# A list schedule's key for TensorE products that use a part of the array

## Chip, cores and metric

The kernel runs on one core of one Trainium2 chip. The metric is the device time of one execution in microseconds (us); lower is better. Times before are the median, the lowest and the highest of three runs.

## What is computed

A decoder of four layers, each with a self-attention block, a cross-attention block and a feed-forward block, on 32 sequences of 64 tokens (2048 tokens of 256 float32 values) and a context of 128 values a token. Every block has the form x = x + f(layernorm(x)), and the twelve f differ:

```python
x = x + _L0_attn_ref(_layernorm(x), wq, wk, wv, wo, ...)        # rope attention, 32 heads of 64, 8 kv heads
x = x + _L0_xattn_ref(_layernorm(x), ctx_1024, mask, ...)       # 16 heads of 128 on the context
x = x + _L0_ffn_ref(_layernorm(x), ...)                         # relu^2 dense and a mixed projection
x = x + _L1_attn_ref(_layernorm(x), ...)                        # Mamba-2 mixer, 32 heads
x = x + _L1_xattn_ref(_layernorm(x), ctx_1024, ...)             # 16 heads of 128, q and k normed
x = x + _L1_ffn_ref(_layernorm(x), ...)                         # 8 experts, top 2
x = x + _L2_attn_ref(_layernorm(x), ...)                        # Mamba-2 mixer, 8 heads
x = x + _L2_xattn_ref(_layernorm(x), ctx_1024, ...)             # 16 heads of 16
x = x + _L2_ffn_ref(_layernorm(x), ...)                         # one binarized projection
x = x + _L3_attn_ref(_layernorm(x), ...)                        # fp4-quantized, 32 heads of 8
x = x + _L3_xattn_ref(_layernorm(x), ctx_1024, pos, ...)        # axial rope, 32 heads of 8
x = x + _L3_ffn_ref(_layernorm(x), ...)                         # 64 experts, top 6, capacity 128, and a shared one
```

## The kernel before

**Tiles and stages.** The tokens stand in SBUF as 16 tiles of 128 (two sequences each). A unit works one block on one tile, or on a pair of tiles. `GROUPS = (8, 6, 2)` splits the tiles into three groups. `body` records the stages so that the early, wide stages of one group are woven (`weave`) with the late, narrow stages of the group before; the first group's early stages have nothing beside them, and the last group's late ones run beside the queued experts of layer 3. Every operation is only recorded: `Recorder.add` notes the engines that could run it, the tiles that it reads and writes, and so on whom it depends.

**The planner.** `Order.run` then decides, by list scheduling with its own table of durations (`duration`), which operation goes next and on which engine; `issue` writes out the instructions in that order. All instructions of the profile therefore carry one line, L2411, and are told apart by the names of their tiles. The order is fixed before the kernel runs: each engine takes its instructions strictly in it and waits on semaphores.

In each step `run` looks, for each engine, at the first 32 ready operations in the order of recording, gives each a key, and takes the lowest key over all engines (the earlier recorded one if keys are equal). The names that matter:

- `now` is when the engine is free, `since` when the inputs and a free slot are there, `start` the later of both.
- `o.soft` is the readiness plus a margin, if an input comes from another engine: `SLACK = {"tensor": 2.0, "vector": 0.5, ...}` us. The plain key is `max(now, o.soft, since)`. So an operation whose input has only just been planned is passed over while another has waited longer.
- `part` rounds the contraction and the output rows of a product up to 32, 64 or 128: the rows and columns of TensorE's 128x128 array that it uses. `self.part` is the part of the last product planned. A product of another part has `SWITCH = 0.1` us added to key and cost.
- `self.pos[o.at]` is the place of an operation in the recorded order, in us of planned TensorE work. `first` is the place of the oldest product that could start now. A product of the set part over `NEAR = 10` us behind `first` has `SWITCH` added to its key too.
- `fill` puts in a product that nobody reads (`spare_mm`) where TensorE would idle for over 1.6 us. `may_open` sees to it that buffers do not run out. PSUM has 8 slots, tag `mm`.

**Products that use a part.** Scores and outputs of attention heads are small, and several lie beside each other in the array:

- 128\*64: `cross_scores` (32 products a tile), `small_values`, `heads_mm` and the outputs of small heads
- 64\*64: `cross_out`, the outputs of L0's attention, `ssm_heads_mm` (32 products a group of heads)
- 32\*128: the scores of L0's attention (64 products a tile); 32\*64: `small_scores`
- 128\*32: sums of squares for L1's cross-attention and the mixers, the experts of layer 3

Their inputs come from ACT and DVE, piece by piece: `cross_out`, for one, takes each half of the transposed probabilities when it has been copied out of PSUM into `turn_b`.

Of the kernel before, what the change touches and what calls it, by code (L numbers as in the profile page):

```python
# [462 lines left out]
def duration(engine, method, args, kw):  # L463

    out = kw["out"] if "out" in kw else args[0]
    if method in DMA:
        return 0.45 if engine == "sync" else 1.28
    views = [v for v in [*args, *kw.values()] if isinstance(v, View)]
    n = max(v.size() for v in views)
    if engine == "tensor":  # L470
        k, m = part(method, args)
        if method == "transpose":
            return 0.109
        n = args[2].size()
        if m == 128:
            return max(0.223, n * 0.00167 + 0.004) if k > 32 else max(0.056, n * 0.00053)
        if k == 128:
            return max(0.058, n * 0.00083 + 0.003) if m == 64 else max(0.055, n * 0.00043 + 0.008)
        return n * 0.00042 + 0.002 if k == 64 else n * 0.00021 + 0.001
    small = any(v.size() == 1 and v.n > 1 for v in views) and n > 1  # L480
    psum = any(v.t.psum for v in views)
    full = sum(all(s for s, _ in v.dims) and v.size() == n for v in views[1:])
    if engine == "vector":
        if not psum and method in ("tensor_scalar", "tensor_copy", "tensor_scalar_add", "tensor_single_scalar"):
            return 0.16 + n * 0.00052 + 0.11 * small
        if method.startswith("reduce") and views[1].dims[-1][0] > 1:
            return 0.15 + n * 0.0017
        return 0.15 + n * 0.00104 + 0.06 * small
    if engine == "scalar":
        if method == "activation":  # L490
            return (0.17 if psum else 0.205) + n * 0.00083 + 0.18 * (small and psum)
        return 0.16 + n * 0.00084 + 0.1 * small
    if method == "memset":
        return 0.2 + n * 0.00066
    if ALU.pow in args:
        return 0.4 + 0.157 * n
    if method == "tensor_copy":
        return 0.25 + n * 0.001
    return 0.14 + n * (0.00174 if full < 2 else 0.0022)
# [27 lines left out]
class Order:  # L527
# [81 lines left out]
    def run(self):  # L609
        ready = {e: [] for e in self.ENGINES}  # L610

        def enter(op):
            for e, _ in op.ways:
                bisect.insort(ready[e], op, key=lambda o: o.at)

        for o in self.ops:
            if o.waits == 0:
                enter(o)
        done, oldest, result = [False] * len(self.ops), 0, []
        while not all(done[oldest:]):  # L620
            limit = self.pos[oldest] + self.horizon
            best = None
            for e in self.ENGINES:
                now, seen, first = self.free_at[e], 0, 1e9
                for o in ready[e]:
                    if self.pos[o.at] > limit or seen == 32:
                        break
                    seen += 1
                    since = o.ready
                    opens = [t for t in o.tiles if t.slot is None and t.tag in self.slots]  # L630
                    if opens:
                        if any(not self.free[t.tag] for t in opens):
                            continue
                        since = max([since] + [self.free[t.tag][0][0] for t in opens])
                    start = max(now, since)
                    method = next(m for w, m in o.ways if w == e)
                    cost = duration(e, method, o.args, o.kw)
                    key = max(now, o.soft, since)
                    if e == "tensor":
                        if start == now:  # L640
                            first = min(first, self.pos[o.at])
                        if part(method, o.args) != self.part:
                            key += SWITCH
                            cost += SWITCH
                        elif self.pos[o.at] > first + NEAR:
                            key += SWITCH
                    if e == "scalar":
                        table = TABLES.get(getattr(o.args[2], "name", "") if method == "activation" else "", 0)
                        if table and table != self.table:
                            key += 1.3  # L650
                            cost += 1.3
                    if e == "vector" and self.until["gpsimd"] > start and combines(o, e, method):
                        cost += min((1 - BESIDE) * (self.until["gpsimd"] - start), cost / BESIDE - cost)
                    if len(o.ways) > 1 and self.elsewhere(o, e, since, start + cost):
                        continue
                    if best is not None and (key, o.at) >= best[0] and not (
                        o is best[1] and start + cost < best[3] + best[4]
                    ):
                        continue
                    if opens and not self.may_open(o):  # L660
                        continue
                    best = ((key, o.at), o, e, start, cost, opens)
                    if key <= now:
                        break
            assert best is not None, "nothing can go on"
            _, o, e, start, cost, opens = best
            filler = self.fill(o, start) if e == "tensor" else None
            if filler:
                o, start, opens = filler, self.free_at[e], []
                cost = duration(e, "matmul", o.args, o.kw)  # L670
            else:
                for w, _ in o.ways:
                    ready[w].remove(o)
            for t in opens:
                t.slot = self.free[t.tag].pop(0)[1]
            got = start + cost
            end = got if o.ways[0][1] in DMA else got - EARLY.get(e, 0.0)
            self.free_at[e] = end
            m = next(m for w, m in o.ways if w == e)
            if combines(o, e, m):  # L680
                self.until[e] = got
                if e == "gpsimd" and self.until["vector"] > start:
                    more = min(self.until["vector"] - start, cost) * (1 / BESIDE - 1)
                    self.free_at["vector"] += more
                    self.until["vector"] += more
            elif e in self.until:
                self.until[e] = 0.0
            if e == "scalar":
                m = next(m for w, m in o.ways if w == e)
                table = TABLES.get(getattr(o.args[2], "name", "") if m == "activation" else "", 0)  # L690
                self.table = table or self.table
            if e == "tensor":
                self.part = part(o.ways[0][1], o.args)
            lat = latency(e, o)
            if o.ways[0][1] in DMA:
                v = next(v for v in o.outs + o.ins if isinstance(v, View) and v.dtype != I32)
                self.moved = max(self.moved, got) + v.n * v.size() * 4 / 300e3
                lat = 2.0 + self.moved - got
            for t in o.tiles:
                t.left -= 1  # L700
                if t.left == 0 and t.tag in self.slots:
                    bisect.insort(self.free[t.tag], (got + lat, t.slot))
            for n in o.after:
                same = len(n.ways) == 1 and n.ways[0][0] == e and o.ways[0][1] not in DMA
                at = (start if e in ("tensor", "sync") else got + 0.03) if same else got + lat
                n.ready = max(n.ready, at)
                n.soft = max(n.soft, at if same else at + SLACK.get(n.ways[0][0], 0.0))
                n.waits -= 1
                if n.waits == 0:
                    enter(n)  # L710
            if not filler:
                done[o.at] = True
            while oldest < len(done) and done[oldest]:
                oldest += 1
            oldest = min(oldest, len(done) - 1)
            result.append((o, e))
        self.length = max(self.free_at.values())
        return result
# [1791 lines left out]
```

## Time and profile before

| | |
|---|---|
| median of 3 runs | 3109.91 us (3098.72 to 3110.64) |
| profiled execution | 3237.79 us |
| its span, first to last instruction | 3236.0 us |
| mean granted TensorE clock in it | 0.955 |
| TensorE busy, records | 3064.8 us (95%), 26996 |
| DVE, ACT, POOL busy | 66%, 45%, 44% |

The profile is one execution. A float32 product leaves two records on TensorE (PE), a transpose one. PEld is the loading of the stationary operand, which overlaps PE. The timeline merges neighbouring records of one kind: start, length, engine and line, operation, tiles, rows\*columns of the array in use, shape of the moving operand, and how many. Waits are gaps of an engine together with what ended them.

### The profile page before, as it was taken

How to read it: one execution, taken by the hardware profiler on the slowest of the kernel's cores; microseconds unless marked ns; L12 is line 12 of the kernel's file. 1: busy time of each engine (PE TensorE's matmuls, PEld its weight loads, DVE VectorE, ACT ScalarE, POOL GpSimd, SP SyncE). 2: the span in 40 equal slices, each digit the busy share in tenths (PEclk: the TensorE clock that was granted, in tenths of full speed). 3: DMA queues.
4: the chain of work that ended last, by engine and by line, in shares of the span. 5: the costliest groups of instructions: out<-in, count | busy, mean ns of one | idle time of the engine just before them, and what ended most of it. 6: DMA issues, size and time to landing. Idle time of an engine off the chain costs nothing.

```text
span 3236.0 us, 66753 instructions
## 1 busy us (share of the span) xinstructions
PE 3064.8 (95%) x26996; PEld 2440.0 (75%) x26996; DVE 2122.1 (66%) x5175; ACT 1452.6 (45%) x2696; POOL 1424.3 (44%) x1281
## 2 busy tenths in 40 slices
PE   8999999999999999999999999989999999987779
PEld 7878887777777787788777776667778777765557
DVE  5554357775556666755789876767547788685474
ACT  1224226675442232544565664653335665363341
POOL 4532143225544555226564465644434575353420
PEclk9989999999998998999999999998899999898689
DMA  4102320121521443111110100112561211222441
GB/s 152 33 3 118 127 77 25 51 82 56 217 88 44 128 152 102 50 44 55 33 34 23 63 5 20 70 55 86 175 226 50 74 53 49 77 77 83 128 158 37
DMA packets 112951, 257.01 MB, mean 79 GB/s; under 512 B 26309, under 2 KB 73688, under 8 KB 100228
## 3 DMA queue, kind: packets, MB, share of 16 engines
q1 hardware_dynamic: 97860, 204.73, 18.3%
q0 software_dynamic: 14784, 48.01, 4.4%
q8 instruction: 214, 3.51, 0.5%
q14 instruction: 93, 0.76, 0.1%
HBM read 177.34 MB, written 78.77 MB: 79 GB/s over the span
## 4 chain that ended last, share of the span: by engine, by line
PE 80%; DVE 9%; issue 3%; POOL 3%; ACT 2%; DMA 1%; another core or an unknown queue 1%; SPq 0%; DVEq 0%; ACTq 0%; POOLq 0%
PE L_xattn_mm L2411 13%; PE L_attn_mm L2411 9%; PE cross_out_mm L2411 9%; PE ssm_heads_mm L2411 9%; PE pair_mm L2411 8%; PE L_ffn_mm L2411 5%; PE rope_mm L2411 4%; PE turn_mm L2411 4%; PE L_block_mm L2411 3%; PE cross_scores_mm L2411 2%; PE L_experts_mm L2411 2%; DVE ssm_heads_b L2411 2%; PE L_dense_mm L2411 2%; PE heads_mm L2411 2%; PE small_scores_mm L2411 1%
## 5 line engine op out<-in xcount | busy, mean ns | idle before, releaser
L2411 PE MATMUL pair_mm<-norm_b,load_ssm_w 128*128 128x256 f32 x1280 | 307.4, 385 | 0.0
L2411 PEld LDWEIGHTS pair_mm<-norm_b,load_ssm_w 128*128 128x128 f32 x1280 | 236.3, 191 | 43.0 <-issue 9.7
L2411 ACT COPY turn_b<-turn_mm 128x512 f32<-128x512 f32 x259 | 143.1, 592 | 203.9 <-PE turn_mm L2411 186.7
L2411 ACT ACT_TABLE_LOAD x165 | 211.7, 1283 | 19.5 <-DVE ssm_heads_b L2411 4.0
L2411 POOL TENSOR_TENSOR norm_sm<-norm_sm,__init___consts 128x1 f32<-128x1 f32 (+1 forms) x142 | 89.5, 635 | 287.0 <-DVE norm_sm L2411 268.8
L2411 DVE SCALAR_TENSOR_TENSOR ssm_heads_b<-pair_mm,load_ssm_wp,ssm_heads_b 128x252 f32<-128x252 f32 (+2 forms) x480 | 198.2, 465 | 20.7 <-ACT ssm_heads_b L2411 19.0
L2411 POOL TENSOR_TENSOR L_xattn_sm<-L_xattn_sm,__init___consts 128x8 f32<-128x8 f32 (+2 forms) x62 | 179.6, 2904 | 69.5 <-DVE L_xattn_sm L2411 50.6
L2411 ACT COPY L_xattn_b<-L_xattn_mm 128x512 f32<-128x512 f32 x191 | 112.2, 590 | 216.8 <-PE L_xattn_mm L2411 213.7
L2411 PE MATMUL rope_mm<-norm_b,load_L_attn_w 128*128 128x128 f32 x1280 | 163.4, 283 | 2.1 <-DMA load_L_attn_w<-in_a_wk 1.2
L2411 PEld LDWEIGHTS rope_mm<-norm_b,load_L_attn_w 128*128 128x128 f32 x1280 | 154.3, 196 | 11.0 <-issue 6.1
L2411 PE MATMUL ssm_heads_mm<-load_ssm_w,ssm_heads_b 128*128 128x256 f32 x640 | 157.0, 387 | 0.3 <-DVE ssm_heads_b L2411 0.3
L2411 POOL TENSOR_TENSOR ssm_heads_b<-ssm_heads_b,ssm_heads_b 128x1024 f32<-128x1024 f32 x30 | 76.1, 2536 | 166.3 <-DVE ssm_heads_b L2411 141.5
L2411 PEld LDWEIGHTS ssm_heads_mm<-load_ssm_w,ssm_heads_b 128*128 128x128 f32 x640 | 117.4, 190 | 34.3 <-issue 19.2
L2411 DVE TENSOR_SCALAR norm_b<-__init___x,norm_sm,norm_sm 128x256 f32<-128x256 f32 x192 | 111.8, 599 | 47.8 <-POOL norm_sm L2411 26.1
L2411 DVE TENSOR_TENSOR rope_b<-rope_mm,__init___consts 128x512 f32<-128x512 f32 x160 | 104.9, 680 | 54.2 <-POOL L_attn_b L2411 14.7
L2411 PEld LDWEIGHTS L_xattn_mm<-norm_b,load_L_xattn_w 128*128 128x128 f32 x1024 | 123.0, 195 | 14.1 <-issue 10.1
L2411 PE MATMUL L_attn_mm<-load_L_attn_w,L_attn_b 128*128 128x256 f32 x512 | 126.9, 401 | 5.8 <-issue 5.6
L2411 PE MATMUL L_xattn_mm<-norm_b,load_L_xattn_w 128*128 128x128 f32 x1024 | 130.3, 281 | 1.2 <-issue 0.8
L2411 POOL DMA_INDIRECT slots<-norm_b,L_ffn_sm x84 | 87.7, 1044 | 96.7 <-issue 44.5
L2411 ACT ACTIVATE ssm_heads_b<-ssm_heads_b 128x512 f32<-128x512 f32 (+1 forms) x120 | 91.8, 772 | 78.5 <-DVE ssm_heads_b L2411 50.5
L2411 POOL TENSOR_TENSOR L_attn_b<-rope_b 128x256 f32<-128x256 f32 x128 | 92.7, 742 | 77.1 <-DVE rope_b L2411 41.0
L2411 PE MATMUL L_xattn_mm<-norm_b,units_L_xattn_w 128*128 128x128 f32 x1024 | 124.2, 278 | 0.0
(440 smaller groups left out, 7935.6 us busy)
## 6 DMA issues: line engine op xcount, KB each, us to landing
queue<-far_w SPq DMA_DIRECT2D x14, 1024.0 KB
L_block_w<-in_f_rows SPq DMA_DIRECT2D x16, 770.0 KB
load_ssm_w<-in_s_in SPq DMA_DIRECT2D x12, 1024.0 KB
parts<-far_w SPq DMA_DIRECT2D x10, 1024.0 KB
slots<-far_w SPq DMA_DIRECT2D x16, 548.0 KB
L_experts_b<-slots SPq DMA_DIRECT2D x32, 274.0 KB
units_L_xattn_w<-kept_x SPq DMA_DIRECT2D x8, 1024.0 KB
L_parts_b<-parts SPq DMA_DIRECT2D x14, 512.0 KB
```

Of the source, the lines that this page charges most:

```text
L2411: done = getattr(getattr(nc, e), method)(*map(real, op.args), **{k: real(v) for k, v in op.kw.items()})
```

## The change

One branch is added to the key of TensorE's products: a product of the part that is set, if it is no more than `NEAR` behind `first` and the part is not the whole array, gets its bare `start` as its key, so without the margin of `SLACK`. Nothing else is touched; operations, durations, slots and the keys of other engines stay.

```diff
                         if part(method, o.args) != self.part:
                             key += SWITCH
                             cost += SWITCH
                         elif self.pos[o.at] > first + NEAR:
                             key += SWITCH
+                        elif self.part != (128, 128):
+                            key = start
                     if e == "scalar":
```

## The prediction

> **What bounds the kernel now.** I read the page's busy times first, then the slices, then the chain, then TensorE's waits, and last its timeline.
>
> ```profile
> PE 3064.8 (95%) x26996; PEld 2440.0 (75%) x26996; DVE 2122.1 (66%) x5175; ACT 1452.6 (45%) x2696; POOL 1424.3 (44%) x1281
> PE   8999999999999999999999999989999999987779
> PEclk9989999999998998999999999998899999898689
> PE 80%; DVE 9%; issue 3%; POOL 3%; ACT 2%; DMA 1%; another core or an unknown queue 1%; SPq 0%; DVEq 0%; ACTq 0%; POOLq 0%
> ```
>
> TensorE is busy for 95% of the span and carries 80% of the chain that ended last; no other engine passes 66%. In the table of stretches it is busy for 1954.8 of the first 2000 us, for 746.1 of the next 800 and for 363.9 of the last 436. So in most of the span a nanosecond taken from TensorE's queue is taken from the end, and in the last 436 us only about five in six are. Its waits are small and scattered:
>
> ```profile
> PE L_experts_mm L2411 <- ACT L_experts_b L2411: 12.9, 5, 4.7
> PE norm_mm L2411 <- DVE norm_b L2411: 11.8, 7, 8.3
> PE turn_mm L2411 <- ACT heads_b L2411: 9.3, 7, 3.4
> ...
> PE small_scores_mm L2411 <- ACT keys_apart_b L2411: 5.5, 5, 2.2
> ```
>
> (total us, times, longest). All gaps of over 150 ns between TensorE's products add to 138 us; 48 of these stand ahead of products that use a part of the array. What remains to be gained is inside the 95%: how the products follow each other. The timeline shows it:
>
> ```profile
> 956.20 1.06 PE L2411 MATMUL L_xattn_mm<-L_xattn_b,__init___consts 128*32 128x512 f32 x6
> 957.19 0.77 PE L2411 MATMUL norm_mm<-__init___consts,norm_b 128*128 128x128 f32 x5
> 957.89 1.04 PE L2411 MATMUL L_xattn_mm<-L_xattn_b,__init___consts 128*32 128x512 f32 x2
> 958.87 0.44 PE L2411 MATMUL norm_mm<-__init___consts,norm_b 128*128 128x128 f32 x2
> 959.23 1.20 PE L2411 MATMUL cross_scores_mm<-L_xattn_b,L_xattn_b 128*64 128x64 f32 x32
> 960.36 0.33 PE L2411 MATMUL norm_mm<-__init___consts,norm_b 128*128 128x128 f32 x1
> 960.62 1.20 PE L2411 MATMUL cross_scores_mm<-L_xattn_b,L_xattn_b 128*64 128x64 f32 x32
> ```
>
> 128\*32 is rows\*columns of the array in use, the last number the records (a float32 product leaves two, a transpose one). Four products of 128\*32 belong together; three run, norm transposes of the full array come between, and the fourth follows. One lone transpose stands between two batches of cross_scores. Each such **break** changes the array's part twice.
>
> **The price of a change of part.** I took the distance from one record's start to the next over the whole timeline. After a 128x128 record of the full array the median is 109 ns if the next record uses the full array (6492 cases), 202 to 205 ns if it uses a part. After a 128x256 record it is 216 ns (5389 cases) against 309. Going back, 128x128 records of 128\*64 are left after 203 ns, and 128x256 ones of 128\*32 after 309. So a change costs 93 ns whatever the parts, and a break 2 x 93 = 0.187 us. In the order of issue there are 1121 changes: 1121 x 0.093 = 104 us, 3.2% of the span. The planner's own SWITCH is 0.1 us.
>
> **What the Trainium skill says.** "TensorEngine Tiling (Array Packing)", Tiling Modes, Key Properties: "Changing tiling mode (not just tile) drains the TensorE". The trace agrees and prices it at 93 ns. "TensorE: Matmul & The Clock Gate", Part 3, on what overlaps: products start and end strictly in program order, so a product that waits holds all behind it; the records here start in the order of issue, save neighbours a few ns apart. The same page, Part 1: an idle window of about 3.4 us can drop the clock. The page's mean granted clock is 0.955, and a late evacuation here costs waits of 0.3 to 3 us, so I charge no clock to the change.
>
> **The change, part by part.** It adds and removes no instruction: the same 26996 TensorE records, the same loads, weight loads, evacuations and DMAs. It alters the order that the planner writes out. Before, a product's key is its readiness plus a margin of 2 us if another engine made its input (SLACK), so within these 2 us a full-array product, at a penalty of only 0.1, is taken first, and the part is left. Now, while a part other than the full one is set, a product of this part that lies within 10 us of recorded TensorE work of the oldest product that could start (NEAR) has its bare start as key: it goes on at once.
>
> *How many breaks can close.* In the order of issue 194 breaks have the same part back within 2.2 us. I then followed the kernel's dependences through the trace for every return to a part: in 223 cases the planner's readiness of the first returning product lies before the end of the run that had been left; in the trace all but 4 of these inputs were indeed there, and those 4 were late by 2.6 us together. But NEAR bites: in 124 of the 223 an older stage has a product startable that lies more than 10 us back (typically 20 to 25, up to 110, since two streams of tiles are woven). 99 keep the new key, and in 78 of them the whole returning run does. By 400 us of the span these 78 are 17, 7, 8, 6, 8, 8, 9 and, to the end, 15: everywhere.
>
> *The sum.* 78 x 0.187 = 14.6 us. The 21 that return in part still change twice: nothing. A run that is lengthened by a half to one us sees further products become ready; I take a quarter more, 3.6 us (bounds: 0, and all 194 short breaks, 194 x 0.187 = 36 us in all). Scores and outputs that finish a batch earlier free their PSUM banks and start the softmax earlier; of TensorE's 138 us of gaps I take 2%, 3 us (bounds: 0 and 15). Against it:
>
> - *The lost margin.* Products now issue with nothing between planned readiness and turn. By the trace, where the old plan left 0.1 to 0.5 us, a quarter of the products had less than 0.28 us left and one in twenty none; where it left over 2 us nearly none waited. The 4 late of 223 give 2.6 x 99/223 = 1.2 us; products that get ready inside the run are worse known, and I add 2 us (bounds: 0 and 40, below). Queued behind such a product is all of TensorE, and behind it ACT's and DVE's evacuations.
> - *The full-array products pushed back* by up to 1 us keep their own margin of 2 us and feed engines that are 45% and 66% busy: nothing. Where that cover is missing, in the last 436 us, the chain goes through DVE and ACT and a push costs what it lasts: 15 breaks x at most 0.5 us, of which I take none, as much is finished earlier as later.
> - *DMA queues, SP and POOL*: their instructions are placed by other keys and move only with the plan; no load is late in TensorE's waits but one of 1.2 us. Nothing.
>
> Sum: -14.6 - 3.6 - 3 + 3.2 = -18 us. The profiled execution took 3237.8 us (span 3236.0), 4% over the median of the runs, 3109.91; the saving is in TensorE's cycles and I carry it over unscaled: 3109.9 - 18 = **3092 us**, -0.6%. About 0.5% (15.5 us) is what a measurement of this kernel can tell from no change; its three runs spread over 12 us.
>
> **The rivals.** *Runs that grow.* If each lengthened run meets the next piece and the oldest startable product moves up because batches finish, NEAR excludes less and most of the 194 short breaks close: -36, with the gaps -45: 3065. For it: 194 of the breaks are short. Against: the older stream's products keep becoming ready one by one.
>
> *Little closes, or the plan gives it back.* A list schedule answers a local gain with another order everywhere. If NEAR excludes as counted, no run grows and the plan's idle time rises by 8 us: -14.6 + 3.2 + 8 = -3: 3106. That the change hardly does what it says is this case.
>
> *Slower: TensorE waits for evacuations.* Place: the second half of a batch right behind its ACT or DVE copy (turn_b into L_attn_mm and cross_out_mm, ssm_heads_b into ssm_heads_mm, L_experts_b into L_experts_mm), where the margin had hidden the copy's own queue. Price: before products that the old plan gave less than 0.1 us after their inputs, the trace has 98 gaps of over 150 ns, 88 us in all, so 0.9 us each. The gain of 18 is gone from 20 such waits on, one in five closed breaks; 40 make +18 and, with an order that is worse in the last 436 us, +22: 3132. Against it: 4 late of 223. For it: a plan with no margin there has not been seen in this trace.
>
> **How the numbers follow.** The forecast case 0.43, its own range 3080 to 3103; runs that grow 0.15; little closes 0.24; slower 0.18. Faster by over 0.5%: three quarters of the forecast and the runs that grow, 0.33 + 0.15 = 0.48. Within 0.5%: the rest of the forecast and nearly all of the third, 0.32. Slower: 0.18 and what the third has beyond, 0.20. The range reaches from a little past the growing runs with the full bound for the gaps (-51) to the slower case: 3055 to 3135.
>
> **What would show it.** Right: in the changed kernel's timeline the changes of part fall from 1121 to 900 to 970, runs of 128\*64, 64\*64 and 128\*32 get longer (now 26, 26 and 8 records), TensorE's busy time falls by 15 to 20 us, and its waits on ACT rise by less than 5. Wrong on the count: fewer than 80 or more than 300 changes gone. Wrong on the margin: waits of cross_out_mm, L_attn_mm or ssm_heads_mm on ACT and DVE that grow by 20 us or more. Wrong on the rest: changes gone as forecast, busy time down, and the span not.

## The result, and the profile after

The changed kernel takes **3057.78 us** (3054.86 to 3059.14, four runs); the kernel before, run beside it, 3106.36. The ratio is 0.9844, with a 95% interval of 0.9824 to 0.9865: 48.6 us or 1.6% faster. The forecast was 18 us. The direction was right and the time lies inside the stated range, but the size was off by a factor of 2.7.

Where a kernel ran matters for the numbers below: beside the changed kernel and e1 to e4 the kernel before took about 3106 us, beside e5 to e18 about 3225, so every ratio is to the kernel before run beside it and profiles are compared only within one of these two sets. The profile that the prediction reads (3237.8 us) belongs with e5 to e18, the profile after with e1 to e4; e1 below is therefore a second profile of the kernel before. The two then read, e1 first (span, busy time, PE's slices and the granted clock):

```profile
span 3107.2 us, 66753 instructions
PE 3004.8 (97%) x26996; PEld 2405.3 (77%) x26996; DVE 2120.7 (68%) x5175; ACT 1450.7 (47%) x2696; POOL 1427.3 (46%) x1281
PE   8999999999999999999999999999999999998989
PEclk9989999999999899999999999999899999899989
```

and after:

```profile
span 3053.1 us, 66780 instructions
PE 2959.3 (97%) x27012; PEld 2401.8 (79%) x27012; DVE 2119.0 (69%) x5186; ACT 1443.4 (47%) x2690; POOL 1411.6 (46%) x1273
PE   8999999999999999999998999999999999998889
PEclk9989999999999999999999999999899999999999
```

The work is the same: 26996 records and eight more spare products of two records each. The span falls by 54.1 us, and PE's busy time alone by 45.5. So TensorE was not freed of waits in the first place; it does the same products in less time. DVE, ACT and POOL hardly differ. In PEclk there are 2 eights instead of 5; in the records the granted clock is either 1 or 0.5, and within the span it stood at 0.5 for 167 us in e1 and 143 us after.

Counted in the order of issue, changes of part fall from 1121 to 996. By the page's groups of TensorE (tiles, part, shape, records, busy us and mean ns), the two groups that fall most are the output of L0's attention and a sum of squares in L1's cross-attention, each with e1 first:

```profile
L2411 PE MATMUL L_attn_mm<-turn_b,L_attn_b 64*64 64x256 f32 x512 | 61.9, 433 | 7.0 <-ACT L_attn_b L2411 4.3 <-DVE L_block_b L2411 2.7
```

```profile
L2413 PE MATMUL L_attn_mm<-turn_b,L_attn_b 64*64 64x256 f32 x512 | 43.7, 396 | 0.2 <-DVE rope_b L2413 0.2
```

```profile
L2411 PE MATMUL L_xattn_mm<-L_xattn_b,__init___consts 128*32 128x512 f32 x128 | 39.9, 605 | 0.0
```

```profile
L2413 PE MATMUL L_xattn_mm<-L_xattn_b,__init___consts 128*32 128x512 f32 x128 | 32.6, 605 | 0.0
```

In the first, the same 512 records take 18.2 us less. By the times of the halved clock, 9.1 us of the 61.9 and 2.4 of the 43.7 are lost to it, so 11.6 us are left that have to do with the order. The timelines of the two show how. In e1:

```profile
55.83 0.65 PE L2411 MATMUL L_attn_mm<-L_attn_b,L_attn_b 32*128 32x64 f32 x10
56.42 0.65 PE L2411 MATMUL L_attn_mm<-turn_b,L_attn_b 64*64 64x256 f32 x4
57.00 0.67 PE L2411 MATMUL L_attn_mm<-L_attn_b,L_attn_b 32*128 32x64 f32 x16
57.60 1.09 PE L2411 MATMUL L_attn_mm<-turn_b,L_attn_b 64*64 64x256 f32 x12
58.62 0.66 PE L2411 MATMUL L_attn_mm<-L_attn_b,L_attn_b 32*128 32x64 f32 x12
59.21 0.78 PE L2411 MATMUL L_attn_mm<-turn_b,L_attn_b 64*64 64x256 f32 x4
...
60.28 1.09 PE L2411 MATMUL L_attn_mm<-turn_b,L_attn_b 64*64 64x256 f32 x12
61.30 0.67 PE L2411 MATMUL L_attn_mm<-L_attn_b,L_attn_b 32*128 32x64 f32 x16
```

and after:

```profile
53.90 0.65 PE L2413 MATMUL L_attn_mm<-L_attn_b,L_attn_b 32*128 32x64 f32 x10
54.48 2.85 PE L2413 MATMUL L_attn_mm<-turn_b,L_attn_b 64*64 64x256 f32 x32
57.26 1.56 PE L2413 MATMUL L_attn_mm<-L_attn_b,L_attn_b 32*128 32x64 f32 x46
```

The 32 records of 64\*64 stood in four pieces that took 0.65 + 1.09 + 0.78 + 1.09 us, between scores of 32\*128; now they are one run of 2.85 us, and the scores are one run too. The break was not only against the full array but between two small parts.

The second group falls by 7.3 us, none of it halved clock. Its records stand in 38 runs in e1 and 31 after. The timeline that the prediction shows has the reason: three products of 128\*32 (6 records) took 1.06 us, and the fourth, alone (2 records), 1.04. In both traces a run of two, four, six or eight records takes 1.04 to 1.07 us. The four write to different columns of the array, so a product that comes with its batch costs next to nothing, and one that comes alone costs the time of the batch.

### The profile page after: what moved, and what is told of

It is laid out like the page before. It is cut to its first block, busy times and chain, and to the rows that moved or that the text cites. A ratio compares the mean times of both kernels' runs of the same rounds, so it can differ in the third digit from the quotient of the medians.

```text
span 3053.1 us, 66780 instructions
## 1 busy us (share of the span) xinstructions
PE 2959.3 (97%) x27012; PEld 2401.8 (79%) x27012; DVE 2119.0 (69%) x5186; ACT 1443.4 (47%) x2690; POOL 1411.6 (46%) x1273
## 5 line engine op out<-in xcount | busy, mean ns | idle before, releaser
L2413 POOL TENSOR_TENSOR L_xattn_sm<-L_xattn_sm,__init___consts 128x8 f32<-128x8 f32 (+2 forms) x62 | 179.1, 2896 | 30.2 <-DVE L_xattn_sm L2413 28.9
L2413 POOL TENSOR_TENSOR ssm_heads_b<-ssm_heads_b,ssm_heads_b 128x1024 f32<-128x1024 f32 x28 | 69.8, 2494 | 159.9 <-DVE ssm_heads_b L2413 130.2
L2413 POOL TENSOR_TENSOR heads_b<-heads_b,heads_sm 128x1024 f32<-128x1024 f32 x50 | 95.8, 1923 | 72.8 <-DVE heads_sm L2413 70.1
L2413 PEld LDWEIGHTS L_xattn_mm<-norm_b,units_L_xattn_w 128*128 128x128 f32 x1024 | 117.8, 192 | 5.8 <-issue 3.8
```

Source lines behind the costliest of these rows:

```text
L2413: done = getattr(getattr(nc, e), method)(*map(real, op.args), **{k: real(v) for k, v in op.kw.items()})
```

## The experiments

### e1: the kernel before, a second profile

No edit. 

> The kernel before, word for word, for a second profile: the first one's span (3236 us) lies 4% over the median of its runs, at a mean granted clock of 0.955, and can't be laid beside the span after (3053 us, 0.977). Theory 1 (what is gained beyond the changes of part is TensorE waiting less): the gaps of over 150 ns stay near 138 us, against 81 after. Theory 2 (the first profile was a slow execution, and its gaps with it): a span of 3090 to 3110 us, a clock of 0.97 to 0.98, and gaps of 80 to 110 us.

It took 3109.0 us, span 3107.2. The gaps of over 150 ns between products are 89 us instead of the 138 of the first profile. Theory 2 holds: a good third of the gaps that the prediction read belong to where that profile was taken. Against 80.9 us after, TensorE's gaps explain 8 us of the gain and no more.

### e2: breaks closed by hand

```diff
+def close(order, far=2.2):      # while a run v of q's part is planned to start within 2.2 us of q's end,
+                                # with u between, and v's inputs and slots are planned before q ends:
...
+            new = before + v + u + [o for r in runs[k + 1 :] for o in r]
+            if merged(new):     # the other engines' orders as they are, and no cycle
+                pe = new
-    issue(tc, order.run(), Net.SLOTS)
+    issue(tc, close(order.run()), Net.SLOTS)
```

> The order of the kernel before, in which 127 breaks are closed after planning: the returning run is put right behind the run that it continues, if all its inputs from other engines and its slots are planned to be there, and the full-array products between come after it. Nothing else moves; DVE, ACT, POOL and SP keep their order. Changes of part 889 instead of 1121. If a change costs 93 ns and the lost margin nothing: 232 x 0.093 = 21.6 us less, a ratio of 0.993. If the drain is hidden or products wait without their margin: 0.998 to 1.005. If the gain after comes from closed breaks and whatever else they bring by themselves (it was 48.6 us for 125 changes, 0.39 us each), this kernel gains 90 us: 0.971.

3059.5 us, a ratio of 0.9842 (0.9813 to 0.9872): 47 us for 232 changes, 0.20 us each and not 0.093. The reordering on TensorE alone, with no new plan, is enough for a gain of this size. Gaps rose by 14 us (to 103.5): giving up the margin does cost, but little. So either the price of a change was wrong or closed breaks bring something more, and e5 measures the price.

### e5: the price of a change by itself

```diff
+        for visits in (1, 20, 40, 80):
+            for v in range(visits):
+                for k in range(160 // visits):
+                    full(k)
+                for k in range(320 // visits):
+                    small(k)
```

> The kernel before, with four stretches of products behind its last one that nobody reads. Each stretch has the same 160 products of the full array (128 columns moving) and the same 320 of 64x64 (64 moving, four places of the array in turn), in 1, 20, 40 and 80 visits to the small part: 1 or 2, 40, 80 and 160 changes of part in all. Nothing in them waits for another engine. If a change costs the 93 ns that I read off the step across it, the last stretch is 158 x 0.093 = 14.7 us longer than the first. If it costs what the closed breaks gave back, 0.2 us, 32 us longer, and the 20 and 40 visits lie 8 and 16 us above the first. In between, the difference is the waits or the clock.

The four stretches as windows (length, then PE and PEld busy with records; next to nothing runs on the other engines, and the clock is full):

```profile
3221.20:3273.67 52.47, 46.31 (x961) 45.58 (x959) 0.42 (x1) 0.00 (x0) 0.00 (x0) 1.00 0.03 10
3273.67:3325.81 52.14, 52.14 (x966) 48.38 (x961) 0.00 (x0) 0.00 (x0) 0.00 (x0) 1.00 0.01 3
3325.81:3385.01 59.20, 59.20 (x966) 51.68 (x961) 0.00 (x0) 0.00 (x0) 0.00 (x0) 1.00 0.01 2
3385.01:3458.40 73.39, 73.39 (x965) 58.32 (x960) 0.00 (x0) 0.00 (x0) 0.00 (x0) 1.00 0.01 2
```

From 20 to 40 visits 7.06 us, from 40 to 80 14.19: **0.354 us a visit, 0.177 a change** (in the expectations after this run: 0.178). The steps between records in the second stretch show what I left out. The step into the small part is 205 ns instead of 112, which I had (+93). The step back is 148 ns, where the small run's own are 7, 7, 7, 38 (+110 against the 38 in its place; I had 93 for it). But then the first full-array record is followed by the second after 213 ns instead of 112 (+101), and the first four small products are followed by the next after 87 instead of 38 (+49). The price lies in two steps across the change and in two more, a product or four later. Sum 353 ns.

This is the price for 64\*64 against the full array. Of the other parts the trace of e1 shows one of the later steps: after a return, whatever part was left, the second full-array record follows the first after 320 ns at the median instead of 216 (256 columns moving, 189 cases) and after 165 to 213 instead of 111 (128 columns, 255 cases). That every change costs 0.178 us, those between two small parts too, remains an assumption of the account below.

The first stretch is longer than 20 visits should make it, though its PE is busy for only 46.31. Its timeline says why:

```profile
3257.02 2.54 PE L2432 MATMUL price<-__init___consts 64*64 64x64 f32 x154
3260.77 2.10 PE L2432 MATMUL price<-__init___consts 64*64 64x64 f32 x128 [1.21 <-issue]
3264.51 2.10 PE L2432 MATMUL price<-__init___consts 64*64 64x64 f32 x128 [1.65 <-issue]
```

A run of nothing but small products stops for 1.65 us after every 128 records, waiting for nothing that the profile shows. Longer runs are not free of limit.

### e17: what else a break costs

```diff
+        for way in (0, 1, 2):
+            for v in range(40):
+                half(0)                        # four products on rows 0 to 63
+                if way == 1:
+                    full(4)
+                half(0 if way == 2 else 1)     # four on rows 64 to 127, or again on 0 to 63
+                full(4 if way == 1 else 8)
```

> The kernel before, with three stretches of products behind its last one that nobody reads, each of 320 products 64x64 (256 moving) and 320 of the full array (128 moving), in 40 rounds. First way: four small products on rows 0 to 63, four on rows 64 to 127, eight full ones. Second: four small, four full, four small, four full, so a round has two more changes. Third: as the first, but all eight small ones on rows 0 to 63. If a change's price is all that a break costs, the second is 40 x 2 x 0.178 = 14 us longer than the first and the third as long as the first. If batches on different rows run beside each other when nothing stands between them, the third is some 40 x 0.85 = 34 us longer than the first (four products, two side by side[...]), and the second up to 48.

```profile
3215.80:3336.57 120.77, 120.77 (x1282) 96.60 (x1281) 0.42 (x1) 0.00 (x0) 0.00 (x0) 1.00 0.02 5
3336.57:3504.50 167.93, 167.93 (x1281) 115.31 (x1281) 0.00 (x0) 0.00 (x0) 0.00 (x0) 1.00 0.00 1
3504.50:3658.80 154.30, 154.30 (x1281) 115.69 (x1280) 0.00 (x0) 0.00 (x0) 0.00 (x0) 1.00 0.00 1
```

The third way, with no more changes than the first, is 33.5 us longer: 0.84 us a round. The timelines of the three ways, in order, have eight small products on both halves in 1.11 us, four on one half in 1.08, and eight on the same half in 1.94:

```profile
3300.34 1.11 PE L2434 MATMUL beside<-__init___consts 64*64 64x256 f32 x16
```

```profile
3401.64 1.08 PE L2434 MATMUL beside<-__init___consts 64*64 64x256 f32 x8
```

```profile
3550.77 1.94 PE L2434 MATMUL beside<-__init___consts 64*64 64x256 f32 x16
```

Batches on different rows run beside each other, on the same rows one after the other. The second way is 47.2 us longer: 1.18 us a round, of which 0.84 is the lost company and 0.34 the two changes (0.17 each, as in e5). The Trainium skill, "TensorE: Matmul & The Clock Gate", Part 3, says that small products at different places of the array run concurrently; this trace agrees, with these numbers. A batch of L0's output for one sequence sits on 64 rows, the other sequence's on the other 64. A break that parts two such batches costs not 0.19 us but, with four products to a batch as here, 1.18.

### e18: only the breaks of 64x64 closed

The edit is e2's, with one line of `close` changed:

```diff
-            if kind(v[0]) != kind(q[0]) or kind(v[0]) == (128, 128) or id(v[0]) in tried:
+            if kind(v[0]) != kind(q[0]) or kind(v[0]) != (64, 64) or id(v[0]) in tried:
```

> As e2, with breaks of the part 64x64 alone closed by hand: 1088 changes of part instead of 1121. By the price of a change alone: 33 x 0.178 = 6 us, a ratio of 0.998. If in the closed breaks the two batches then run beside each other: up to 17 x 0.85 = 14 us more, 0.993 to 0.996.

0.9969 (0.9955 to 0.9984), about 10 us of 3225 for 33 changes. The price alone gives 5.9 us, 0.9982, which lies just inside the interval; the forecast with the company was 0.993 to 0.996, just below the mean. The group of L0's output:

```profile
L2412 PE MATMUL L_attn_mm<-turn_b,L_attn_b 64*64 64x256 f32 x512 | 52.0, 415 | 7.3 <-ACT L_attn_b L2412 4.6 <-DVE L_block_b L2412 2.7
```

It was 61.2 in the first profile before: 9.2 us less, 7.1 of them at full clock. It stands in 36 runs instead of 51, of which the price explains some 2.4 us (0.16 us of a visit falls into the small products), so 4 to 5 us are company. The time of the whole kernel cannot tell the two forecasts apart; the group speaks for the company, but for less of it than the 14 us allowed.

### e3, e4 and e7 to e12: neighbours of both kernels

Four pairs, each the kernel before and the changed one with the same small edit, for the luck of an order:

```diff
-SLACK = {"tensor": 2.0, ...}      # e3, e4: 2.05     e11, e12: 1.95
-NEAR = 10                         # e7, e8: 9        e9, e10: 11
```

> The changed kernel with TensorE's margin 2.05 us instead of 2.0, a neighbour that has no reason of its own to be faster or slower; 983 changes of part against 996. Theory A (all of the gain belongs to the new key): 3050 to 3065 us, a ratio of 0.982 to 0.987. Theory B (11.6 us belong to the changes of part, the rest is the luck of one order among many): 3070 to 3100, 0.988 to 0.998.

> The kernel before with the margin 2.05 us; 1105 changes of part against 1121. Theory A: 3100 to 3112 us, a ratio of 0.998 to 1.002. Theory B: anything from 3080 to 3130, and with e3 a difference between the pair of 10 to 15 us rather than 48.

> The kernel before with NEAR 9 instead of 10; 1106 changes of part. A neighbour for the spread of orders: theory A (the key is worth 50 us in every pair) 3095 to 3125 and e8 about 50 below; theory B (20 to 25 us from the changes, the rest luck) anything from 3080 to 3130, and e8 at most 30 below.

> The changed kernel with NEAR 9; 976 changes of part, 130 fewer than e7. Theory A: 50 us below e7. Theory B: 130 x 0.2 = 26 us below e7, give or take 20 for the luck of the order.

> The kernel before with NEAR 11; 1107 changes of part. With e10, e11 and e12 two more pairs of neighbours that differ by the new key alone; three pairs so far gave 1.56% (the kernels themselves), 1.8% (margin 2.05) and 0.14% (NEAR 9). Theory A (the key is worth about 50 us in every order, the pair with NEAR 9 is the exception): 0.99 to 1.005 here, the partner 1.6% below. Theory B (the changes of part at the 0.178 us of e5, the rest the luck of an order): 0.985 to 1.01 here, the partner 0.8% below, give or take 0.8%.

> The changed kernel with NEAR 11; 960 changes of part, 147 fewer than e9: 147 x 0.178 = 26 us, 0.84%. Theory A: 1.6% below e9. Theory B: 0 to 1.6% below e9, and the mean over the five pairs nearer to 0.9% than to 1.6%.

> The kernel before with TensorE's margin 1.95 us; 1099 changes of part. Theory A: 0.995 to 1.005. Theory B: 0.985 to 1.01.

> The changed kernel with the margin 1.95 us; 959 changes of part, 140 fewer than e11: 25 us, 0.8%. Theory A: 1.6% below e11. Theory B: as for e10; it can be no faster than e11 at all.

| pair | without the key | with the key | changes of part | gain of the key |
|---|---|---|---|---|
| the kernels themselves | 1 | 0.9844 (0.9824 to 0.9865) | 1121, 996 | 1.6% |
| margin 2.05 (e4, e3) | 1.0085 (1.0055 to 1.0116) | 0.9908 (0.9875 to 0.9941) | 1105, 983 | 1.8% |
| NEAR 9 (e7, e8) | 0.9950 (0.9928 to 0.9972) | 0.9936 (0.9921 to 0.9951) | 1106, 976 | 0.1% |
| NEAR 11 (e9, e10) | 1.0011 (0.9998 to 1.0024) | 0.9930 (0.9905 to 0.9955) | 1107, 960 | 0.8% |
| margin 1.95 (e11, e12) | 0.9962 (0.9944 to 0.9979) | 0.9931 (0.9911 to 0.9951) | 1099, 959 | 0.3% |

The mean of the five is 0.9%, some 29 us, for 122 to 147 changes: 0.178 us each make 22 to 26 of it. Theory A, 1.6% in every pair, has fallen; with NEAR 9 the intervals of the two kernels nearly coincide. Theory B holds as e9 puts it, with the measured price. As first put in e3 and e4 it missed: that pair differs by 55.6 us where it had 10 to 15, and e4 lies above every range. The key is worth about 0.9%, and a given order gets more or less by about as much again. What took it back in the profiles of e7 and e8 are waits: the gaps between products add to 122.7 and 133.6 us, and those inside a product, between its two records, to 15.7 and 22.7, though 130 changes are gone. The largest of e8's waits (total us, times, longest):

```profile
PE L_attn_mm L2413 <- issue: 17.2, 23, 2.4
PE L_experts_mm L2413 <- issue: 12.3, 18, 2.8
PE norm_mm L2413 <- DVE norm_b L2413: 11.0, 6, 8.2
PE cross_out_mm L2413 <- issue: 9.8, 9, 4.8
```

All waits on "issue" together are 46 us in e7 and 66 in e8, three quarters of them in front of small products. These are single profiles: in the other two pairs run beside 3225 us they went from 43 to 40 (e9, e10) and from 29 to 38 (e11, e12), so that the key brings them is not shown. In e1 to e4 and after they were 1 to 3 us.

### e13: the changed kernel again

No edit. 

> The changed kernel, word for word, beside kernels that ran where the kernel before took 3225 us instead of 3106. Price theory: 125 changes of part x 0.178 = 22 us of its 48.6 belong to the key, and the rest to what TensorE waits for; where it waits for its own instructions (29 to 66 us in the profiles of e6 to e12, 1 to 3 in the others) the gain is smaller: 0.988 to 0.993 there, 0.984 again where it doesn't. Theory A (the key is worth 1.6% in its own pair everywhere): 0.984 on either.

3177.3 us beside 3224.6, a ratio of 0.9841 (0.9807 to 0.9876). The suspicion that the gain depends on where it runs has fallen: it is the same, and the pairs differ because their orders do.

### e14 and e15: the measured price given to the planner

```diff
-SWITCH = 0.1
+SWITCH = 0.18
```

> The kernel before with SWITCH 0.18, the price of a change that e5 measured, instead of 0.1; no new key. 1069 changes instead of 1121: 52 x 0.178 = 9 us. If knowing the price also lets the planner time the other engines rightly: 10 us more, 0.992 to 0.995. If the key is what counts: 0.996 to 1.003.

> The changed kernel with SWITCH 0.18; 977 changes, 19 fewer than with 0.1: 3 us below e13 by the price alone, and 10 to 15 below if the truer price makes a better plan.

1.0037 (1.0024 to 1.0051) and 0.9907 (0.9870 to 0.9943). Neither is better than with 0.1: the true price in the planner's account didn't make a better order. e15 is 18 us slower than e13; e14 lost although it has 52 changes fewer; its gaps between products are 161.6 us against 138 before. As a pair the key is worth 1.3%.

### e6 and e16: the changed kernel with the remaining breaks closed

`close` as in e2, on the changed kernel and on e15. 

> The changed kernel, and in its order the breaks that remain short are closed by hand as in e2: 863 changes of part instead of 996. At 0.093 us: 12 us below the changed kernel, 3045. At the 0.2 us of e2: 27 us below, 3031, a ratio of 0.976 to the kernel before. If the margin that the changed kernel gave up was the last that could be: 3055 to 3070.

> As e15, with the breaks that remain short closed by hand as in e2 and e6; 867 changes, 110 fewer than e15: 20 us below it by the price, less 5 to 10 us of added waits; 0.970 to 0.978 of the kernel before, the fastest of all. If waits give all of it back: as e15.

e6 is the fastest of all: 0.9763 (0.9735 to 0.9792), 0.8% below the changed kernel (e13: 0.9841) for 133 changes fewer, 25 us where the price gives 24. e16 missed: 0.9893 (0.9861 to 0.9924), only 6 us below e15 in the medians for 110 changes, which the intervals don't tell from nothing. Its gaps between products are 7 us longer than e15's and 10 us more go to the halved clock. Why closing brought more waits there than in e6 was not followed further.

## Why the prediction was right or wrong

The account, from e1 and the profile after. Gaps are those over 150 ns between records; the clock's share is half of the time at 0.5 that is no gap; a spare product counts two steps of 216 ns.

| | e1 | after | difference |
|---|---|---|---|
| gaps | 89.3 | 80.9 | -8.4 |
| lost to the halved clock | 76.5 | 66.6 | -9.9 |
| changes x 0.178 | 199.5 | 177.3 | -22.2 |
| spare products | 28.9 | 32.4 | +3.5 |
| all other | 2709.8 | 2692.6 | -17.2 |
| end of TensorE's last product | 3104.0 | 3049.8 | -54.2 |

Between the first profile before and e13, both run beside 3225 us, the same lines give -18.2, -4.2, -22.2, +3.5 and -13.2, in all -54.3 us.

- **What bounds the kernel** was right: but for eight spare products nothing was added or taken away, what shrank was time on TensorE, and it came off the end.
- **The price of a break** failed: 0.187 us against 0.354. I took the step across the change for the whole. The steps after the return and after the start of the small run were left out, though the records of the trace had them. (The median step between full-array records of 128 columns is 111 ns in it, not 109, which changes nothing here.)
- **The count** failed the other way: 78 whole closings and a quarter more would be 195 changes fewer; 125 are gone, below the 151 to 221 of "from 1121 to 900 to 970". Too many closings at half the price: 18.2 us forecast for this part, 22.2 measured. That the two errors nearly cancel is luck, and they do not explain why the forecast was too small.
- **A term was missing**, and this is the step that made 18 us out of some 50: the sum has nothing for products that run beside each other when they come together. At full clock, the group of L0's output falls by 11.6 us with 24 runs fewer (51 to 27), and the group of 128\*32 by 7.3 with 7 fewer. The price puts some 0.16 us of each visit into such groups, 3.8 and 1.1 us; the rest, some 14 us, I put down to company, in the first group on different rows of the array, in the second on different columns. e17 shows the mechanism for rows, e18 its trace in the kernel; for columns the lengths of the runs show it. The prediction had both in hand, the rows in the program (`rb` for each sequence) and, for the columns, the lines of 1.06 and 1.04 us in its own timeline, and priced neither.
- **How far company fills "all other"** is argued, not shown. In the five pairs, in the order of the table above, L0's group at full clock falls by 11.6, 7.6, 6.2, 5.1 and 7.8 us and that of 128\*32 by 7.3, 6.2, 0.9, 5.0 and 6.3. So every pair has company, but "all other" moves by -17.2, +0.5, +2.0, -5.6 and -14.3. With the margin 2.05 the groups of cross_out (64\*64) and small_scores (32\*64) take it back, by 4.9 and 6.0 us; with NEAR 9 what does so is open.
- **The gaps** fell by 8.4 us where I took 3 and then gave 3.2 back. The lost margin, feared most, costs 14 us for 232 changes in e2 and nothing that shows in the changed kernel.
- **The clock** was charged at nothing, and it gave 4 to 10 us. The ground was that the waits stay below the idle window of about 3.4 us that the prediction cites. But in e1 no gap after the first product is longer than 3.3 us, after none is longer than 2.6, and the clock was halved in 20 and 18 stretches all the same: by these traces, shorter gaps go with it too. Fewer breaks went with less of it: in e2, with the fewest breaks among e1 to e4, the time at half clock is 130 us against 167 in e1; from the kernel without the key to the one with it the time falls by 24, 48, 28 and 25 us in the first four pairs of the table, by nothing with the margin 1.95, and by 17 in e14 and e15. Against it stands e16, with 31 us more than e15. That fewer breaks raise the clock is likely by these numbers and was not isolated.
- **The rivals.** "Runs that grow" had the size (-45) for the wrong reason: short breaks did not close more often, each was worth more. "Slower by waiting for evacuations" did not come; where a neighbour lost its gain (e8) the waits that had grown were on "issue". "The plan gives it back" is what the pairs show, by up to 20 us.

Of the 54 us between the two profiles, then, 22 are changes of part at the price of e5, some 14 company in the array, and 18 clock and gaps, which belong to this order as much as to the key: five pairs give the key 29 us on the mean.

## What to carry to other kernels

Price a change of the array's part over the whole visit, from the last product before to the second one after, and not by the step across: here 0.35 us a visit instead of 0.19. Keep products that use different rows or columns of the array together, since such a one costs its full time alone and next to nothing beside its partners. A timeline shows it at a glance: runs of one product and of four that take the same time. And where a planner writes the order, measure a change to it in several neighbours: one pair here says 1.8% and another 0.1%.

## What was not expected of the hardware

- A visit to a 64x64 part costs 0.354 us, so a change 0.177: 93 ns in the step into the part, 49 after the first four small products, 110 in the step back, and 101 in the step after the first full-array record (e5).
- Four 64x64 products of 256 columns on rows 0 to 63 take 1.08 us, and with four more on rows 64 to 127 1.11; on the same rows eight take 1.94 (e17).
- One to four products of 128\*32 with 512 columns, on different columns of the array, take 1.04 to 1.07 us (e1 and after).
- A long run of 64x64 products (64 columns) stops for 1.65 us after every 128 records (e5).
- The granted clock knows two values in these traces, 1 and 0.5, and was halved 18 times in a run with no gap over 2.6 us after its first product (after).
